# Expert products in 64-row tiles of TensorE, issued in pieces of at most 128 columns

## The chip, the cores and the metric

The kernel runs on one core of a Trainium2 chip. A core has TensorE (PE in the profile; its weight loads are listed apart as PEld), VectorE (DVE), ScalarE (ACT), GpSimd (POOL) and SyncE (SP, which issues most DMAs). The metric is the device time of one execution in microseconds (us), as the median of several runs. Before the change it is 1270.68 us (three runs, 1270.43 to 1271.75).

## The reference, cut to what matters

One transformer block on 2048 tokens of 512 numbers, all in fp32. The result is the sum of three terms: the input, an attention branch and a branch of experts, both fed by the layer-normed input.

```
xn  = layernorm(x)
attention: 16 heads, each with two causal softmax maps; a filter along the tokens; RMS norm; @ Wout
experts:   the gate picks 2 of 8 experts for each token
           routed:  y_e = (silu(xn @ w1[e]) * (xn @ w3[e])) @ w2[e]      (512 -> 352 -> 512)
           shared:  y_s = (silu(xn @ sw1) * (xn @ sw3)) @ sw2            (512 -> 704 -> 512)
out = x + attention + routed (weighted by the gate) + shared
```

Only the order in which the experts' products are issued to TensorE is touched by the change; what is computed is the same.

## The kernel before

The program goes through four stages. First it normalises the tokens, turns them (`xnT`, features on partitions), computes the values `vd`, the gate, the routing and the rotated queries and keys. Then comes `middle`, the longest stage: attention, with the experts' products worked in between. Then `ending` applies the filter, the norm and `Wout`, and gathers the experts' rows. There are two versions of `middle` (lines 1600 to 1605); with the data given, the one without a running maximum runs (`middle(False)`).

**The order of the work in `middle`** is written out by hand: the string `PLAN` (lines 63 to 83) has a letter for each step, and lines 1314 to 1319 carry them out. `S` computes the scores of one unit (line 1067, two matmuls of 64 rows each, for the two maps), after which ScalarE takes the exponential (line 1080) and GpSimd masks the diagonal blocks (line 1089). `V` multiplies the probabilities with the values (line 1111). `U` and `F` sum up and finish a chunk of queries. A lower-case `a` adds probabilities on VectorE (line 1127). `W` advances the experts by one step: `experts` (line 736) is a generator and `W` runs it to its next `yield`. The scores have two PSUM buffers, so a score unit waits for the exponential of the unit but one before it.

**The experts' products** go through `crossing` (line 691). TensorE is used there as two halves: rows 0 to 63 of the contraction (`LO`) and rows 64 to 127 (`HI`) are separate matmuls of 64 rows. Two products are made together, each in a PSUM bank of its own. In a first pass (`n == 0`) the `LO` rows go to the first product while the `HI` rows go to the second. In a second pass (`n == 1`) they change places, so that each product gets both halves, and the two halves never write the same bank at once. Between the passes stands a wait: a ScalarE nop waits for the last matmul of each half of the first pass, and the first matmul of each half in the second pass waits for the nop (`behind`, lines 684 to 689; lines 715 to 719). `passes` (line 726) cuts a crossing into `W` steps of `step` products.

`run(n, a, b)`, line 705, issues the matmuls from product `a` to `b` of a pass: for each `k` one matmul of the `LO` half and one of the `HI` half, with all the columns that the product has. The callers and their moving columns are:

- `wh`, the shared expert's hidden products (line 766): stationary 64 x 128 weights, moving `xnT` with 512 tokens, or 384 in the last group; the sixth chunk has 256, and 256 beside 128 in the last group. One `k` a step.
- `wy`, the shared expert's output (line 826): stationary activations, moving weights with 512 columns, or 256 where a tile is alone. One `k` a step.
- `xu`, a routed expert's hidden products (line 909): stationary 64 x 128 or 64 x 96 weights, moving 128 tokens. Four `k` a step.
- `xy`, a routed expert's output (line 930): moving weights with 256 columns. All three `k` of a pass a step.

In the profile each of these fp32 matmuls appears as two MATMUL rows with two LDWEIGHTS rows. The routed rows come in 34 tiles of 128 slots. 28 of them belong to a single expert and go through `crossing`; six are shared by two experts and go through other functions (`up_half`, line 206, and `down_products`, line 240), which are not touched. The weights of the routed experts are fetched by SyncE into two sets of buffers (`fetch`, `refill`, line 879), each part as soon as TensorE has last read the one before.

Of the kernel before, what the change touches and what calls it, by code (L numbers as in the profile page):

```python
# [20 lines left out]
P = 128  # L21
# [24 lines left out]
LO, HI = slice(0, HALF), slice(HALF, P)  # L46
# [54 lines left out]
def block_kernel(  # L101
# [240 lines left out]
    with ExitStack() as pools:  # L342
# [94 lines left out]
        for c in range(NE):  # L437
            for i in range(NQC):
                nc.tensor.matmul(
                    gt_ps[32 * i : 32 * i + 32, 0, :], gw_sb[:, c, :], xnT[:, c, i * QC : (i + 1) * QC],  # L440
                    start=(c == 0), stop=(c == NE - 1), skip_group_check=True,
# [41 lines left out]
        for t in range(NT):  # L483
# [5 lines left out]
                start=False, stop=(t == NT - 1), skip_group_check=True,  # L489
# [49 lines left out]
        pairs = l1.tile([P, TOP, NT, 2], F32, name="pairs")  # L539
# [27 lines left out]
        _, _, _, _, chunks, _, result = shared_expert(ep, eps)  # L567
# [15 lines left out]
        for st in range(2):  # L583
            for qk in (1, 0):
                if (st, qk) == (1, 1):
                    load_wqk(1, 0, nc.sync)
                for n in range(NQC):
                    cols = slice(n * QC, (n + 1) * QC)
                    ps = lps.tile([P, 2, QC], F32, tag="x", name="ps_x")
                    for i in range(2):  # L590
                        for c in range(NE):
                            nc.tensor.matmul(  # L592
                                ps[:, i, :], wqk_sb[st, qk][:, i, c, :], xnT[:, c, cols],
                                start=(c == 0), stop=(c == NE - 1),
# [49 lines left out]
    def middle(general):  # L644


        with ExitStack() as pools:
# [18 lines left out]
            def bank(shape, name):  # L666


                n = next(n for n in taken if n not in in_pair)
                taken.remove(n)  # L670
                taken.append(n)
                return f_banks.tile(shape, F32, tag=f"f{n}", name=name)
# [11 lines left out]
            def behind(ins, others):  # L684
                for other in others:
                    tc.add_manual_dep(
                        ins.ins, other.ins.name,
                        mybir.DependencyInfo(mybir.DependencyClass.Sync, mybir.DependencyReason.DATA), reason="the other rows",
                    )

            def crossing(shapes, name, first, second=None):

                banks = []
                for shape in shapes:
                    banks.append(bank(shape, name))
                    in_pair.add(taken[-1])  # L700
                pairs = first(banks), second(banks) if second else first(banks)[::-1]
                whole = [max(map(len, each)) for each in pairs]
                last, signal = [None, None], []

                def run(n, a, b):
                    for k in range(a, b):
                        for i, r in enumerate((LO, HI)):
                            side = pairs[n][i]
                            if k < len(side):
                                dst, lhs, rhs = side[k]  # L710
                                last[i] = nc.tensor.matmul(  # L711
                                    dst, lhs[r], rhs[r], start=(n == 0 and k == 0), stop=(n == 1 and k == len(side) - 1),
                                    skip_group_check=True,
                                )
                                if n == 1 and k == 0:
                                    behind(last[i], signal)
                    if b >= whole[n] and n == 0:
                        signal.append(nc.scalar.nop())
                        behind(signal[0], last)
                    elif b >= whole[n]:  # L720
                        in_pair.clear()
                    return banks

                return run, whole

            def passes(run, whole, step):
# [587 lines left out]
            steps = dict(S=score, V=value, U=sum_up, F=finish, T=lambda: turning[0](), W=work, g=fold_step)  # L1314
# [257 lines left out]
    with tc.If(nc.values_load(more[0:1, 0:1], min_val=0, max_val=1) > 0):  # L1572

        with tc.tile_pool(name="before_more", bufs=1) as gap, tc.tile_pool(name="more", bufs=2) as mp, tc.tile_pool(
# [4 lines left out]
            for j in range(NR, NS):  # L1579
# [6 lines left out]
                pairs = both[:, 0]  # L1586
                nc.vector.tensor_add(pairs, pairs, both[:, 1])
                i = mp.tile([P, 1], I32, tag="i", name="i")
# [121 lines left out]
```

## Time and profile before

| | |
|---|---|
| median of the runs | 1270.68 us |
| the profiled execution | 1267.82 us |
| its span, first to last instruction | 1266.1 us |
| granted TensorE clock, mean | 0.998 |
| TensorE matmuls and weight loads | 10954 of each |
| of them from line 711 | 4200: `xu` 2688, `xy` 672, `wh` 576, `wy` 264 |
| chain that ended last, largest parts | `ps_o` L1111 19%, `ps_s` L1067 12%, `xu` L711 12%, `wh` L711 8%, `xy` L711 5%, `wy` L711 4% |

The rows of line 711 by the number of moving columns: 512 columns 540 (`wh` 320, `wy` 200 and 20), 384 columns 160 (`wh`), 256 columns 796 (`wh` 80, `wy` 40 and 4, `xy` 672), 128 columns 2704 (`xu` 2688, `wh` 16).

How to read the profile: times are in us unless marked ns, and count from the start of the span. L711 is line 711 of the kernel; a matmul that a helper issues carries the helper's line, so `wh`, `wy`, `xu` and `xy` are told apart by the tile that they write. In a listing by line, "64*128 64x512 f32 x320 | 79.0, 591" means 64 rows and 128 stationary columns, 64 x 512 moving numbers, 320 times, 79.0 us busy in all, 591 ns mean length of one. Matmuls overlap, and their ends are modelled: the mean length is not the time that one adds, and a busy TensorE is not TensorE at its peak. In a timeline, instructions of one kind that follow each other are merged: start, length of the whole, engine, line, tile, form, count, and in brackets the idle time before with what ended it. In a table of stretches, each engine's busy time is followed by its number of instructions, then come the granted clock, the DMA share and GB/s. The chain that ended last is followed back from the last instruction, at each step to what released it.

`middle` spans about 253 to 1160 us: the shared expert's products (`wh`, `wy`) lie from 253 to 564 us, the single-expert tiles (`xu`, `xy`) from 567 to about 1010 us and, for the last two, from 1126 to 1155 us; the mixed tiles lie between.

### The profile page before, as it was taken

Reading aid. Unit: us, or ns where it says so; the run is one execution under the profiler, and the core shown is the slowest. Engines: PE = TensorE matmul, PEld = TensorE weight load, DVE = VectorE, ACT = ScalarE, POOL = GpSimd, SP = SyncE. Lnnn points to the kernel's source line nnn. Section 1 sums busy time; section 2 is a strip of 40 time slices with the busy share of each in tenths; the row PEclk is TensorE's granted clock in tenths of the full one; section 3 lists DMA queues with packets and bytes.
Section 4 is the critical chain, followed back from the end, with each engine's and each line's share of the span. In section 5 each row is a group of like instructions: output and inputs, shape, how many; then the busy total and the mean of one; then the engine's idle time right before and its main releaser. Section 6 shows DMA issues by size and latency. Waiting matters only on the chain.

```text
span 1266.1 us, 27950 instructions
## 1 busy us (share of the span) xinstructions
PE 1238.9 (98%) x10954; PEld 704.5 (56%) x10954; DVE 997.9 (79%) x1582; ACT 699.7 (55%) x908; POOL 315.5 (25%) x356
## 2 busy tenths in 40 slices
PE   7999999999999999999999999999999999999998
PEld 3444444444544545566777766767766744456544
DVE  7039886177968878878889999999899897776884
ACT  2311111066756667767777778777777756651331
POOL 0001332011111122111221523222222322111875
PEclk9999999999999999999999999999999999999999
DMA  9505867301130122237566566665665669868998
GB/s 370 215 1 147 219 176 173 105 15 34 47 89 20 28 90 72 83 108 233 171 203 225 194 209 200 211 208 171 201 212 186 200 221 332 297 250 271 188 224 188
DMA packets 85782, 214.75 MB, mean 170 GB/s; under 512 B 16788, under 2 KB 17240, under 8 KB 85384
## 3 DMA queue, kind: packets, MB, share of 16 engines
q1 hardware_dynamic: 72920, 185.70, 45.5%
q0 software_dynamic: 11056, 22.78, 8.7%
q10 hardware_dynamic: 1664, 4.38, 1.1%
q8 instruction: 89, 1.46, 0.5%
q14 instruction: 53, 0.43, 0.1%
HBM read 169.69 MB, written 43.10 MB: 168 GB/s over the span
## 4 chain that ended last, share of the span: by engine, by line
PE 75%; DMA 15%; POOL 4%; issue 2%; DVE 1%; ACT 1%; SPq 0%; ACTq 0%; POOLq 0%; DVEq 0%
PE ps_o L1111 19%; PE ps_s L1067 12%; PE xu L711 12%; DMA who<-pairs,slot 11%; PE wh L711 8%; PE xy L711 5%; PE ps_tv L427 5%; PE wy L711 4%; POOL res L1364 3%; PE ps_sum L1144 2%; DMA res<-ysh 2%; PE ps_x L592 2%; PE xy L244 1%; PE xh L210 1%; PE xg L210 1%
## 5 line engine op out<-in xcount | busy, mean ns | idle before, releaser
L1080 ACT ACTIVATE pt<-ps_s 128x1024 f32<-128x1024 f32 x544 | 537.4, 1026 | 201.6 <-PE ps_s L1067 142.7
L1127 DVE TENSOR_TENSOR sum<-sum,pt 128x1024 f32<-128x1024 f32 (+3 forms) x512 | 515.9, 1057 | 45.5 <-ACT pt L1080 22.7
L1089 POOL TENSOR_SCALAR_AFFINE_SELECT pt<-pt 128x256 f32<-128x256 f32 (+1 forms) x224 | 152.9, 703 | 530.0 <-ACT pt L1080 528.9
L1067 PE MATMUL ps_s<-qS,kS 64*128 64x512 f32 (+3 forms) x1280 | 272.9, 476 | 4.1 <-DVEq L1572 1.7
L1111 PE MATMUL ps_o<-pt,vd 128*32 128x512 f32 (+3 forms) x2560 | 262.2, 533 | 1.5 <-POOL pt L1089 1.5
L1067 PEld LDWEIGHTS ps_s<-qS,kS 64*128 64x128 f32 x1280 | 112.8, 186 | 129.6 <-issue 52.9
L711 PE MATMUL xu<-xT,w 64*128 64x128 f32 (+1 forms) x2688 | 168.3, 272 | 0.0
L711 PEld LDWEIGHTS xu<-xT,w 64*128 64x128 f32 (+1 forms) x2688 | 162.1, 178 | 6.7 <-issue 1.8
L1111 PEld LDWEIGHTS ps_o<-pt,vd 128*32 128x32 f32 x2560 | 70.7, 109 | 121.5 <-issue 104.0
L711 PE MATMUL wh<-xnT,w 64*128 64x512 f32 (+3 forms) x576 | 122.6, 523 | 0.0
L592 PE MATMUL ps_x<-xnT,wqk_sb 128*128 128x512 f32 x256 | 110.5, 593 | 0.0
L1132 DVE TENSOR_TENSOR sum<-pt 128x1024 f32<-128x1024 f32 (+1 forms) x64 | 73.9, 1167 | 45.0 <-ACT pt L1080 26.5
L678 POOL DMA_INDIRECT xrow<-xd,tok x34 | 54.3, 1597 | 146.3 <-PE ps_x L861 123.7
L711 PE MATMUL xy<-w,uT 64*128 64x256 f32 x672 | 83.4, 380 | 0.0
L592 PEld LDWEIGHTS ps_x<-xnT,wqk_sb 128*128 128x128 f32 x256 | 48.4, 190 | 60.6 <-issue 60.6
L545 POOL DMA_INDIRECT who<-pairs,slot x32 | 35.1, 1096 | 168.2 <-DVE pairs L542 103.6
L711 PEld LDWEIGHTS wh<-xnT,w 64*128 64x128 f32 x576 | 56.1, 186 | 26.6 <-issue 17.5
L609 ACT CAST hi<-turned 128x1024 fp32r<-128x1024 f32 x16 | 16.7, 1045 | 93.9 <-DVE turned L607 70.9
L711 PEld LDWEIGHTS xy<-w,uT 64*128 64x128 f32 x672 | 62.8, 187 | 7.7 <-DVE vd L1170 0.6
L1364 POOL DMA_INDIRECT res<-ys,slot x32 | 53.6, 1676 | 23.3 <-DMA res<-ysh 11.6
L427 PE MATMUL ps_tv<-wv_sb,xnT 128*128 128x512 f32 x128 | 58.8, 612 | 0.7 <-ACT xnT L424 0.7
L1507 PE MATMUL po<-wo_sb,aT 128*128 128x512 f32 x120 | 54.1, 593 | 0.2 <-ACT aT L1501 0.2
(247 smaller groups left out, 1180.0 us busy)
## 6 DMA issues: line engine op xcount, KB each, us to landing
w<-in_wex_dram SPq DMA_DIRECT2D x88, 704.0 KB, 7.1
w<-in_wex_dram SPq DMA_DIRECT2D x43, 768.0 KB, 5.8
kS<-parts_k SPq DMA_DIRECT2D x256, 64.0 KB, 2.0
qS<-parts_q SPq DMA_DIRECT2D x256, 64.0 KB, 3.0
ys<-y_sb SPq DMA_DIRECT2D x34, 256.0 KB, 4.1
parts_q<-hi SPq DMA_DIRECT2D x32, 256.0 KB, 5.7
parts_k<-hi SPq DMA_DIRECT2D x16, 256.0 KB, 3.5
parts_k<-turned SPq DMA_DIRECT2D x16, 256.0 KB, 6.0
```

The source lines that it names most:

```text
L427: nc.tensor.matmul(pv, xnT[:, c, t * P : (t + 1) * P], wv_sb[:, c, :], start=(c == 0), stop=(c == NE - 1))
L592: nc.tensor.matmul(ps[:, i, :], wqk_sb[st, qk][:, i, c, :], xnT[:, c, cols], start=(c == 0), stop=(c == NE - 1),)
L678: nc.gpsimd.indirect_dma_start(out=x, out_offset=None, in_=xd, in_offset=bass.IndirectOffsetOnAxis(ap=tok[:, j : j + 1], axis=0),)
L711: last[i] = nc.tensor.matmul(dst, lhs[r], rhs[r], start=(n == 0 and k == 0), stop=(n == 1 and k == len(side) - 1), skip_group_check=True,)
L1067: nc.tensor.matmul(to, k, queries[2 * g + h, qc][r, off : off + w], start=True, stop=not general)
L1080: nc.scalar.activation(pt[:, :, used], ps[:, :, used], AF.Exp, scale=SCALE)
L1089: nc.gpsimd.affine_select(out=part, in_=part, pattern=[[0, part.shape[1]], [1, P]], compare_op=ALU.is_ge, fill=0.0, base=0, channel_multip ...
L1111: nc.tensor.matmul(self.o[r : r + 32, off:], vd[:, kb, v0 : v0 + 32], pt[:, s, :], start=first, stop=self.ended, skip_group_check=True,)
L1127: nc.vector.tensor_add(to, to, pt)
L1132: nc.vector.tensor_add(self.sum[h][:, :, m], self.first[h][:, :, m], pt)
L1364: nc.gpsimd.indirect_dma_start(out=came[k], out_offset=None, in_=ys, in_offset=bass.IndirectOffsetOnAxis(ap=slot[:, step - 2, order[k] : o ...
L1507: nc.tensor.matmul(po, aT[:, c, :], wo_sb[:, c, :], start=(c == 0), stop=(c == NE - 1))
```

## The change

In `run`, each matmul is cut along its moving columns into pieces of at most 128 (`P`). The pieces of the two halves go in turn: `LO` columns 0 to 127, `HI` columns 0 to 127, `LO` columns 128 to 255, and so on; where one half has fewer columns, the other goes on alone. Every piece is a matmul with the same stationary operand as the whole had. `start` is set on the first piece of a half's first product only and `stop` on the last piece of the last; the wait for the nop is put on the first piece of the second pass, and `last` holds the last piece issued. `xu`, which has 128 columns already, is issued as before. `PLAN`, the steps and all other code are the same.

```diff
                 def run(n, a, b):
                     for k in range(a, b):
-                        for i, r in enumerate((LO, HI)):
-                            side = pairs[n][i]
-                            if k < len(side):
-                                dst, lhs, rhs = side[k]
+                        steps = [(i, r, *pairs[n][i][k]) for i, r in enumerate((LO, HI)) if k < len(pairs[n][i])]
+                        for j in range(0, max(rhs.shape[-1] for *_, rhs in steps), P):
+                            for i, r, dst, lhs, rhs in steps:
+                                m = slice(j, min(j + P, rhs.shape[-1]))
+                                if m.start >= m.stop:
+                                    continue
                                 last[i] = nc.tensor.matmul(
-                                    dst, lhs[r], rhs[r], start=(n == 0 and k == 0), stop=(n == 1 and k == len(side) - 1),
+                                    dst[:, m], lhs[r], rhs[r, m], start=(n == 0 and k == 0 and j == 0),
+                                    stop=(n == 1 and k == len(pairs[n][i]) - 1 and m.stop == rhs.shape[-1]),
                                     skip_group_check=True,
                                 )
-                                if n == 1 and k == 0:
+                                if n == 1 and k == 0 and j == 0:
                                     behind(last[i], signal)
```

## The prediction, made before the result was known

> **What bounds the kernel now.** I read the page first, then the stages, then the forms of the changed line, then the matmuls one by one.
>
> The head of the page (engine, busy us, share of the span, instructions) and the chain that ended last:
>
> ```profile
> PE 1238.9 (98%) x10954; PEld 704.5 (56%) x10954; DVE 997.9 (79%) x1582; ACT 699.7 (55%) x908; POOL 315.5 (25%) x356
> ...
> PE 75%; DMA 15%; POOL 4%; issue 2%; DVE 1%; ACT 1%; SPq 0%; ACTq 0%; POOLq 0%; DVEq 0%
> ```
>
> TensorE is busy throughout and the chain lies on it. A busy PE need not be working at its peak, so the stages come next: busy time by engine from 250 to 565 us (shared expert beside attention) and from 565 to 1020 us (routed experts beside attention).
>
> ```profile
> 250.00:565.00 315.00, 311.77 (x2614) 158.53 (x2616) 251.92 (x309) 215.20 (x250) 57.22 (x84) 1.00 0.19 56
> 565.00:1020.00 455.00, 453.14 (x6090) 319.78 (x6082) 413.23 (x690) 337.49 (x455) 126.31 (x146) 1.00 0.63 203
> ```
>
> In both, PE lacks 3.2 and 1.9 us of being always busy, the granted clock is 1.00, and VectorE (252 of 315, 413 of 455) and ScalarE have room. What PE takes longer there, the end gets later by.
>
> The forms of the changed line 711 (rows x stationary columns, then moving rows x columns, count, busy us, mean ns):
>
> ```profile
> L711 PE MATMUL xu<-xT,w 64*128 64x128 f32 x1792 | 114.2, 273 | 0.0
> ...
> L711 PE MATMUL xy<-w,uT 64*128 64x256 f32 x672 | 83.4, 380 | 0.0
> L711 PE MATMUL wh<-xnT,w 64*128 64x512 f32 x320 | 79.0, 591 | 0.0
> L711 PE MATMUL xu<-xT,w 64*96 64x128 f32 x896 | 58.8, 270 | 0.0
> ```
>
> The kernel already holds the form that the change makes of everything: xu, in 128 columns, 1792 times. Each product is two MATMUL rows and each row has its own LDWEIGHTS (10954 of both in all). The durations (591 and 273) overlap, so the price is the pace, read from the timeline (start, length, engine, line, count): a stretch in which score pairs (L1067) and runs of wh alternate, and one in which score pairs and runs of xu do.
>
> ```profile
> 279.67 1.02 PE L711 MATMUL wh<-xnT,w 64*128 64x512 f32 x4
> ...
> 280.75 1.02 PE L711 MATMUL wh<-xnT,w 64*128 64x512 f32 x4
> ...
> 281.84 1.02 PE L711 MATMUL wh<-xnT,w 64*128 64x512 f32 x4
> ```
>
> ```profile
> 654.75 1.05 PE L711 MATMUL xu<-xT,w 64*128 64x128 f32 x16
> ...
> 655.53 0.19 PEld L1067 LDWEIGHTS ps_s<-qS,kS 64*128 64x128 f32 x2
> 655.56 0.48 PE L1067 MATMUL ps_s<-qS,kS 64*128 64x512 f32 x2
> ...
> 655.88 1.04 PE L711 MATMUL xu<-xT,w 64*96 64x128 f32 x16
> ```
>
> Four wh rows of 512 and a score pair take (281.84 - 279.67) / 2 = 1.085 us. Sixteen xu rows of 128, the same number of columns, and a score pair take 655.88 - 654.75 = 1.13 us. That is the change in miniature: 0.045 us more for two pairs of 512, 22 ns a pair (a pair is one row from each half).
>
> **The change part by part.**
>
> *Columns streamed.* The same before and after; the two halves run side by side in both. In a run of wh the loads of successive pairs start at 384.15 and 384.58 us, and those of the score pair behind them at 385.01: 430 ns a pair of 512.
>
> ```profile
> 384.15 0.21 PEld L711 LDWEIGHTS wh<-xnT,w 64*128 64x128 f32 x2 [0.22 <-issue]
> 384.58 0.21 PEld L711 LDWEIGHTS wh<-xnT,w 64*128 64x128 f32 x2 [0.22 <-issue]
> 385.01 0.21 PEld L1067 LDWEIGHTS ps_s<-qS,kS 64*128 64x128 f32 x2 [0.22 <-issue]
> ```
>
> Loads lie idle 0.22 us between pairs ("issue": nothing to wait for but the stream). This slack is what the change fills.
>
> *Instructions added.* Line 711 has 540 rows of 512 columns (wh 320, wy 200 and 20), 160 of 384 (wh) and 796 of 256 (wh 80, wy 44, xy 672). They become 2160, 480 and 1592: 2736 more matmuls and 2736 more loads, each load with the weights that its half already held. xu stays as it is.
>
> *Pace of the pieces.* In the xu run of 16 above, the last of 8 pairs starts (1.05 - 0.27) us after the first (0.27 is the mean row), 0.78 / 7 = 111.5 ns a pair. Loads run without a gap there, so stream and load are about equally long and little hides the rest. Against that:
> - 512: 4 x 111.5 - 430 = 16 ns a pair within a run, 22 with its ends (the 1.13 against 1.085). I take 18; 270 pairs give 4.9 us.
> - 384: a run of 12 wh rows at 476.43 us lasts 2.10 us, less one row (0.49) over 5 steps is 322 ns a pair; 3 x 111.5 - 322 = 12.5 ns, 80 pairs, 1.0 us.
> - 256: loads in xy runs start 215.5 to 217 ns apart (12 rows in 1.46 us, less 0.376, over 5); 2 x 111.5 - 216 = 7 to 7.5 ns, 398 pairs, 3.0 us.
>
> Sum: **8.9 us** of PE time, 6.3 of it before 565 us (wh, wy) and 2.6 after (xy).
>
> *Bounds of the pace.* What no row shows is 128-column pieces that load the same weights again. From below: the xu rows with 96 stationary columns, whose loads are shorter (160 against 188 ns), go 16 rows in 1.04 us, (1.04 - 0.27) / 7 = 110 ns a pair; by that the sum is 270 x 10 + 80 x 8 + 398 x 4 = 4.9 us. Zero would need loads that are left out, and every row has one; that is a rival below. From above: 22 ns for 512 with run ends, and 16 and 10 in proportion for the others: 5.9 + 1.3 + 4.0 = 11.2 us. I stay near the plain 128-column rows, which differ from the new pieces in nothing but the weights.
>
> *A rule against the change.* The trace has 55.8 ns a row of 128 columns and 215 ns a row of 512 (half a pair's pace), nearly a ratio of 4. The Trainium skill, "TensorE: Matmul & The Clock Gate", section "Back-to-back issue gap", gives about 81 ns a matmul sustained at 128 columns and 131 at 512. By that page a row of 512 cut in four would cost 4 x 81 - 131 = 193 ns more, and 540 of them 104 us, as an estimate; no run here shows such a price, and the xu rows speak against it.
>
> *Waits.* The wait between the two passes of a crossing stays on the first piece, and the ScalarE nop still waits for the last; nothing new is queued behind it. Pieces behind the first need no wait, since PE goes in order. The order of all other work and of every DMA stays; weight fetches wait for the last reader on PE, so they move with it.
>
> *What lies beside other work.* PE's idle time in the middle is the cover: 3.2 + 1.9 us by the stages, of which 1.7 lie ahead of the first wide product (253 us) and 0.8 just behind it (256 us), where hardly any delay has built up. Of the remaining 2.6, spots where PE waits for GpSimd's mask or ScalarE's exp, and of the weight wait after 1117 us (which moves along, because PE triggers those fetches), I count 0.6 us as taken up. The tail after 1160 us starts from the last stored expert row and moves along.
>
> **Sum.** 8.9 - 0.6 = +8.3 us. The profiled execution took 1267.82 us (span 1266.1 and 1.7 outside), so the like of it would be 1276.1; it lies 2.9 below the median of the runs, so the forecast stands on that: 1270.68 + 8.3 = **1279.0 us**.
>
> **Rivals.**
> 1. *Repeated weights are cheap.* The program might not reload what a half already holds, or the load might hide. For: no row shows a reload of the same weights. Against: every MATMUL row has its own load. The pieces then cost between nothing and the 4.9 us of the 110 ns pace: 1270.7 to 1275.6, about half of it within what counts as no change.
> 2. *Faster: the halves are not really side by side.* If the ends of the rows (which are modelled) hide that one half of a wide run lags by a row, 430 ns, with the other half of the array idle at its ends, pieces of 128 would cut the lag to 111.5: 0.32 us a run. I count 208 runs of wide products in the timeline, so up to 67 us less: 1279 - 67 = 1212 us. Against it: taking the pairs out of the two periods above leaves 1.085 - 2 x 0.43 = 0.225 us for the score pair beside wh and 1.13 - 8 x 0.1115 = 0.24 beside xu; a lag would leave 0.32 more beside wh. It decides from 8.9 / 208 = 43 ns of lag a run on.
> 3. *Dearer: instructions.* PE gets 25% more of them, 0.35 MB to fetch. The instruction queue carries 1.46 MB in 89 packets of 16 KB now, so 21 more; if each held PE up for 0.5 to 1 us (the size of PE's present waits), +10 to +21 on top: 1289 to 1300. Against: xu runs hold 4 instructions in 111.5 ns, 36 a us, for the 2.7 us of 48 rows without a gap.
>
> **How the numbers follow.** The forecast's case (1276 to 1282): 0.74. Cheap reload: 0.13, of which 0.06 within no change. Faster: 0.05. Dearer: 0.08. The range leaves out the last two and the 0.06: 1273 to 1283, which holds both bounds of the pace (4.9 - 2.6 gives 1273.0, 11.2 gives 1281.9). With 0.2% (2.5 us, about what a measurement of this kernel tells from no change): faster 0.05, same 0.06, slower 0.89.
>
> **What the changed profile would show.** PE at x13690; line 711 with 128 columns only, 6936 rows; pairs 111 to 112 ns apart in wh runs too, with loads that no longer idle 0.22 us; the exp's period beside wh 1.125 instead of 1.085; the shared expert's stage some 6 us longer, the routed one's some 2.5, the mixed pairs and the tail unchanged but later. Wrong would be: fewer loads than matmuls, a wh pace above 115 ns, gaps on PE with no releaser, or a stage before 565 us that gets shorter.

## The result, and the profile after

The changed kernel takes 1280.1 us (median of 6 runs, 1277.46 to 1282.01), the kernel before 1270.05 in the runs beside it: a ratio of 1.0076, 95% interval 1.0062 to 1.0091. That is 10 us more, by the interval 7.9 to 11.6. A second set of runs (below) gives 1.0064 (1.0050 to 1.0077), so the cost is some 8 to 10 us. The forecast was 1279.0, 8.3 over the median it started from.

The profiled execution took 1278.31 us, 1276.6 of it span. The head of its page, and the queue that brings TensorE's instructions among others:

```profile
PE 1247.4 (98%) x13690; PEld 801.3 (63%) x13690; DVE 997.1 (78%) x1582; ACT 699.8 (55%) x908; POOL 312.2 (24%) x356
...
q8 instruction: 111, 1.82, 0.6%
```

There are 2736 more matmuls and as many more loads, and 22 more packets of instructions. VectorE and ScalarE do what they did. TensorE's busy time grew by 8.5 us, that of the loads by 97 us: the loads filled time that had been free.

The two stages with the changed products, cut at the first `wh`, the first `xu` and the first product of a mixed tile (busy us and number of each engine, then clock, DMA share, GB/s). Before:

```profile
253.24:567.12 313.88, 312.39 (x2633) 158.74 (x2631) 252.75 (x308) 215.97 (x251) 57.04 (x82) 1.00 0.19 56
567.12:1020.60 453.48, 451.62 (x6067) 319.14 (x6063) 411.71 (x689) 336.77 (x453) 125.41 (x145) 1.00 0.63 203
```

After:

```profile
254.17:573.54 319.37, 318.10 (x4698) 242.54 (x4697) 252.83 (x309) 216.11 (x251) 56.27 (x82) 1.00 0.20 56
573.54:1028.88 455.34, 453.73 (x6690) 330.97 (x6687) 410.69 (x689) 336.66 (x453) 124.58 (x145) 1.00 0.62 202
```

The shared expert's stage is 5.5 us longer, the routed one's 1.9. In both, PE's busy time grew by a little more than the stage (5.7 and 2.1), while VectorE's, ScalarE's and GpSimd's stayed within 1.1 us: little of the cost was taken up, and PE's idle time did not grow (1.5 and 1.9 us before, 1.3 and 1.6 after). The granted clock is 1.00 in all four.

The price itself, in the timeline after, at the place that corresponds to the stretch at 280 us before (`wh` is issued on line 713 now, the score pairs on line 1070):

```profile
281.19 1.05 PE L713 MATMUL wh<-xnT,w 64*128 64x128 f32 x16
...
282.00 0.47 PE L1070 MATMUL ps_s<-qS,kS 64*128 64x512 f32 x2
282.08 1.09 PEld L713 LDWEIGHTS wh<-xnT,w 64*128 64x128 f32 x16
282.31 1.05 PE L713 MATMUL wh<-xnT,w 64*128 64x128 f32 x16
...
283.43 1.05 PE L713 MATMUL wh<-xnT,w 64*128 64x128 f32 x16
```

Sixteen rows of 128 columns and a score pair now take 1.12 us (281.19, 282.31, 283.43), where four rows of 512 and a score pair took 1.085. The loads run through, 16 in 1.09 us; the 0.22 us in which they lay idle between pairs are gone. The pair of pieces starts every (1.05 - 0.27) / 7 = 111.5 ns, as `xu` does.

### The profile page after: what moved, and what is told of

The parts are those of the page before. It is cut to its first block, busy times and chain, and to the rows that moved or that the text cites. A ratio compares the mean times of both kernels' runs of the same rounds, so it can differ in the third digit from the quotient of the medians.

```text
span 1276.6 us, 33408 instructions
## 1 busy us (share of the span) xinstructions
PE 1247.4 (98%) x13690; PEld 801.3 (63%) x13690; DVE 997.1 (78%) x1582; ACT 699.8 (55%) x908; POOL 312.2 (24%) x356
## 4 chain that ended last, share of the span: by engine, by line
PE 68%; DMA 4%; POOL 4%; issue 2%; DVE 1%; ACT 1%; SPq 0%; POOLq 0%; DVEq 0%; ACTq 0%
PE ps_o L1114 18%; PE ps_s L1070 12%; PE xu L713 12%; PE wh L713 8%; PE xy L713 5%; PE wy L713 4%; POOL res L1367 3%; PE ps_sum L1147 2%; DMA res<-ysh 2%; PE xy L244 1%; PE xh L210 1%; PE xg L210 1%; DMA res<-ys,slot 1%; DMA w<-in_wex_dram 1%; PE ps_x L864 1%
## 5 line engine op out<-in xcount | busy, mean ns | idle before, releaser
L1070 PE MATMUL ps_s<-qS,kS 64*128 64x512 f32 (+3 forms) x1280 | 234.4, 417 | 4.0 <-DVEq L1575 1.7
L1070 PEld LDWEIGHTS ps_s<-qS,kS 64*128 64x128 f32 x1280 | 109.2, 186 | 92.6 <-ACT pt L1083 36.4
L713 PEld LDWEIGHTS wh<-xnT,w 64*128 64x128 f32 x1936 | 124.1, 188 | 5.1 <-issue 0.8
L713 PE MATMUL wh<-xnT,w 64*128 64x128 f32 x1936 | 126.4, 272 | 0.0
L713 PE MATMUL xy<-w,uT 64*128 64x128 f32 x1344 | 85.6, 274 | 0.0
L713 PEld LDWEIGHTS xy<-w,uT 64*128 64x128 f32 x1344 | 81.9, 188 | 2.5 <-DVE vd L1173 0.6
L713 PE MATMUL wy<-w,ws 64*128 64x128 f32 x880 | 55.7, 273 | 0.0
```

Source lines behind the costliest of these rows:

```text
L713: last[i] = nc.tensor.matmul(dst[:, m], lhs[r], rhs[r, m], start=(n == 0 and k == 0 and j == 0), stop=(n == 1 and k == len(pairs[n][i]) - ...
L1070: nc.tensor.matmul(to, k, queries[2 * g + h, qc][r, off : off + w], start=True, stop=not general)
```

## The experiments

For each profile I cut the span at the same six instructions: first `wh`, first `xu`, first mixed-tile product, first `xu` after those, last `xy`, end. All in us; "before" is three profiles (the first one and the two repeats told of below); the second row has the changed kernel's first profile, its repeat, and the run with new weights in each piece.

| kernel | ahead | shared | routed | mixed | last two | tail |
|---|---|---|---|---|---|---|
| before | 253.2, 254.2, 253.9 | 313.9, 314.0, 313.8 | 453.5, 453.5, 453.5 | 105.7, 106.7, 106.4 | 28.0, 28.0, 28.0 | 111.8, 111.9, 113.8 |
| changed; again; new weights | 254.2, 253.1, 254.6 | 319.4, 319.2, 319.4 | 455.3, 455.2, 455.3 | 105.8, 105.7, 106.5 | 28.6, 28.6, 28.6 | 113.3, 113.7, 113.3 |
| pieces of 256 | 254.4 | 314.9 | 453.4 | 107.5 | 28.7 | 112.2 |
| 128 in wh, wy only | 252.9 | 319.4 | 453.3 | 104.3 | 28.4 | 113.9 |
| 128 in xy only | 254.0 | 314.0 | 455.4 | 104.5 | 28.3 | 112.8 |
| one half first | 253.8 | 360.1 | 458.5 | 106.2 | 28.8 | 114.6 |
| 64 in wh, wy | 253.8 | 479.6 | 456.4 | 108.3 | 28.6 | 112.0 |
| two and two | 254.1 | 322.8 | 458.4 | 106.4 | 28.8 | 112.1 |

The stages shared and routed repeat within 0.2 us. The stretches ahead, mixed and tail vary by 1 to 2 us between executions of the kernel before, and by up to 4 across all the rows, so single us of the total are read from the stages.

### The changed kernel again

No edit.

> The changed kernel once more, beside the others. My account (pace: a pair of 128-column pieces takes 111.5 ns where 512 columns took 430 and 256 took 216) gives some 8 us over the kernel before, all of it between the first shared-expert product and the last routed one; the +0.9 us ahead of them and the +1.5 us behind them that the first profile shows would be chance and not come again. If they belong to the change, both come again and the time is 10 us over.

Measured: 1277.3 us, ratio 1.0064 (1.0050 to 1.0077), +7.6 on the medians. The stages repeat (319.2 and 455.2). The 0.9 us ahead did not come again (253.1), the long tail did (113.7).

### Pieces of 256

```diff
+                        wide = 2 * P
-                        for j in range(0, max(rhs.shape[-1] for *_, rhs in steps), P):
+                        for j in range(0, max(rhs.shape[-1] for *_, rhs in steps), wide):
...
-                                m = slice(j, min(j + P, rhs.shape[-1]))
+                                m = slice(j, min(j + wide, rhs.shape[-1]))
```

> Pieces of at most 256 columns in turn, so 540 rows of 512 become 1080 of 256, 160 of 384 become 160 of 256 and 160 of 128, and xy stays whole. Pace: 270 pairs x (2 x 216 - 430) = 0.5 us and 80 x (216 + 111.5 - 322) = 0.4 us, about +1 us over the kernel before. Rival (each added matmul and load costs by its number, as instruction supply would): 700 of 2736 rows are added, 26% of 10 us, +2.6 us.

Measured: 1272.59 us, ratio 1.0021 (1.0013 to 1.0030), +2.9 on the medians, by the interval 1.7 to 3.8. By the total the rival's 2.6 fits better than 1. By the stages it does not: all the added rows lie in the shared stage, which is 1.0 us longer (314.9 against 313.9), as the pace has it. In the changed kernel 2064 added rows make this stage 5.5 us longer; by their number 700 would make it 1.9 longer. The stage repeats within 0.2 us, so this one profile speaks for the pace. The routed stage did not grow (453.4). What the total has beyond 1.0 us lies in the stretches that vary (mixed 107.5) and in the last two tiles (28.7); what brought it there is open.

### 128 columns in wh and wy only, and in xy only

```diff
+                        wide = P if name in ("wh", "wy") else E      # the other run: P if name == "xy" else E
-                        for j in range(0, max(rhs.shape[-1] for *_, rhs in steps), P):
+                        for j in range(0, max(rhs.shape[-1] for *_, rhs in steps), wide):
...
-                                m = slice(j, min(j + P, rhs.shape[-1]))
+                                m = slice(j, min(j + wide, rhs.shape[-1]))
```

> 128-column pieces for wh and wy only; xy keeps 256. Pace: the shared expert's stage is as long as in the changed kernel (319.4 us, 5.5 over before), the routed stage as before (453.5), together +5.5 to +6.3 us. Rival (number of instructions): 2064 of 2736 rows, 75% of 10 us, +7.5 us.

> 128-column pieces for xy only; wh and wy stay whole. Pace: the shared expert's stage as before (313.9 us), the routed stage as in the changed kernel (455.3, 1.9 over before), +2 to +2.6 us in all. Rival (number of instructions): 672 of 2736 rows, 25% of 10 us, +2.5 us; this run alone does not tell them apart, its stages and the sum with the run on wh and wy do.

Measured: 1273.61 us, ratio 1.0034 (1.0021 to 1.0046) for `wh` and `wy`; 1271.39 us, 1.0019 (1.0007 to 1.0031) for `xy`. The stages come out as the account by pace says, each in its place: 319.4 and 453.3 us in the first, 314.0 and 455.4 in the second. The two costs simply add up: 5.5 and 1.9 us by the stages, as in the changed kernel (by the medians 3.9 and 1.7, against 7.6 for the changed kernel in the same set, with intervals of some 3 us each). These two runs do not separate the rivals. The 7.5 us that the number of instructions was said to cost in the first run rest on 10 us for the whole; of the 7.6 in this set 75% are 5.7, inside the interval of 2.7 to 5.8. And by the stages an added row costs 2.7 ns in `wh` and `wy` (5.5 us / 2064) and 2.8 in `xy` (1.9 / 672). It is the runs with pieces of 256 and of 64 that speak against a price per row.

### One half first

```diff
-                        for j in range(0, max(rhs.shape[-1] for *_, rhs in steps), P):
-                            for i, r, dst, lhs, rhs in steps:
+                        cuts = range(0, max(rhs.shape[-1] for *_, rhs in steps), P)
+                        for each in steps:
+                            for j in cuts:
+                                i, r, dst, lhs, rhs = each
```

> Pieces of 128 columns, but all pieces of one half ahead of all of the other instead of in turn. Theory A (TensorE takes its matmuls in program order, a half runs beside the other only where the two follow each other): of 512 columns cut in four, only the last piece of one half and the first of the other can overlap, so a pair of 512 takes up to about 780 ns instead of 446, +90 us on 270 pairs, +16 on 80 pairs of 384 and +45 on 398 of 256: about +150 us over the changed kernel. Theory B (the order within a pair does not matter, because enough pieces are in flight): within 3 us of the changed kernel.

Measured: 1323.36 us, ratio 1.0431 (1.0411 to 1.0452). Both theories fail as they stand. The order matters, by 40.7 us in the shared stage and 3.2 in the routed one. Theory A's sum lets nothing overlap but the two halves of one product; by that the shared stage would lose some 115 us (90, 18 rather than 16 for 384 columns, and 7 for the 62 pairs of 256). But in strict order, too, the last piece of one product can run beside the first of the next (or beside a score pair that stands between). Then a step of 512 columns, two rows for each piece, takes 12 rows' time for 8, one of 384 columns 8 for 6, and one of 256 nothing more: 135 x 4 x 0.1115 + 40 x 2 x 0.1115 = 69 us in the shared stage, and next to nothing for `xy`. So the routed stage does not speak against strict order; the 40.7 us and the starts of the rows do. The timeline (score pairs are on line 1072 here, the pieces on 715):

```profile
284.00 1.27 PE L715 MATMUL wh<-xnT,w 64*128 64x128 f32 x13
285.01 0.50 PE L1072 MATMUL ps_s<-qS,kS 64*128 64x512 f32 x1
285.11 0.50 PE L715 MATMUL wh<-xnT,w 64*128 64x128 f32 x4
285.37 0.48 PE L1072 MATMUL ps_s<-qS,kS 64*128 64x512 f32 x1
285.45 1.16 PE L715 MATMUL wh<-xnT,w 64*128 64x128 f32 x12
```

The two rows of a score pair, which started together, are 0.36 us apart (285.01 and 285.37): one half of TensorE runs ahead by three to four rows. In the single rows of the trace the first product of this stretch starts with 4 rows alone (284.002, 284.115, 284.224 and 284.336), then two rows together (284.448 and 284.453), one alone, two more pairs, and 5 alone. Rows of one half follow each other every 0.11 us, so two that start together lie in different halves. So the second half starts when the first half's third piece does, as its fifth row starts; in strict order it could not start before the fourth piece, the seventh row.

### Pieces of 64

```diff
+                        wide = HALF if name in ("wh", "wy") else P
```

(used as in the run with pieces of 256)

> Pieces of 64 columns for wh and wy, 128 for xy. Theory A (the weight load sets a floor: loads of 128 columns come no closer than some 107 to 112 ns a pair, however short the matmul): a pair of 512 columns takes 8 x 111 = 890 ns instead of 446, +120 us on 270 pairs, +27 on 80 pairs of 384, +14 on 62 of 256, about +160 us over the changed kernel. Theory B (each piece costs its columns, 0.84 ns each, and a fixed 4 ns): a pair of 64 columns takes 58 ns, +5 us over the changed kernel.

Measured: 1446.66 us, ratio 1.1403 (1.1343 to 1.1463); the shared stage is 479.6 us, 160 more than in the changed kernel, as theory A says. The timeline, pieces of half the columns:

```profile
281.69 3.68 PE L714 MATMUL wh<-xnT,w 64*128 64x64 f32 x64
285.18 0.48 PE L1071 MATMUL ps_s<-qS,kS 64*128 64x512 f32 x2
285.49 1.89 PE L714 MATMUL wh<-xnT,w 64*128 64x64 f32 x32
```

32 pairs in 3.68 us, less one row of 0.27, over 31 steps: 110 ns a pair (in the single rows 112, after a first step of 55), the same as with 128 columns. So here the pace does not come from the moving columns. It could come from the loads, or from a fixed price of each row or pair, and other lines of the same profile tell these apart:

```profile
383.01 0.89 PEld L1148 LDWEIGHTS ps_sum<-sum,pick 128*32 128x32 f32 x32
383.12 1.06 PE L1148 MATMUL ps_sum<-sum,pick 128*32 128x128 f32 x32
...
394.56 0.39 PEld L1160 LDWEIGHTS ps_ot<-cst,o_sb 64*128 64x128 f32 x8
394.67 0.42 PE L1160 MATMUL ps_ot<-cst,o_sb 64*128 64x64 f32 x8
```

`ps_sum` takes four rows, each with its own load of 32 columns, in (1.06 - 0.27) / 7 = 113 ns, and `ps_ot` (transposes) two rows of 64 columns in the two halves, with their loads, in some 65 ns. A fixed price of 55 ns a row, or of 110 ns a pair, is refuted. What remains is the load. Its recorded length goes with the stationary columns, 110 ns for 32 (`ps_sum`), 160 for 96 and 188 for 128 (`xu`), which is 0.81 ns a column and an estimate of 104 ns for 128. For these products, then, a pair goes no faster than its two loads, side by side. It is not so for every load of 128 columns: those of the transposes last 138 ns and come every 65.

The Trainium skill, "TensorE: Matmul & The Clock Gate", section "LDWEIGHTS (loading the stationary operand)", has columns / 1.2 ns for a load, by which 128 columns take 107 ns, as an estimate. The 110 to 112 measured for the products here come near it, if the loads of the two halves run side by side; the transposes, at some 65, do not agree with it.

### New weights in each piece

The pieces of `xy` go through the three products of a pass for the first 128 columns, then for the next.

```diff
-                    for k in range(a, b):
+                    cuts = range(0, max(rhs.shape[-1] for side in pairs[n] for *_, rhs in side), P)
+                    for j, k in [(j, k) for j in cuts for k in range(a, b)]:
...
-                        for j in range(0, max(rhs.shape[-1] for *_, rhs in steps), P):
```

> As the changed kernel, but xy, whose three products of a pass stand in one step, goes piece by piece through the three products, so that each load brings other weights than the one before it on its half; wh and wy, with one product a step, are as in the changed kernel. If a repeated load of the same weights costs what any load costs, the time is that of the changed kernel within 1 us and xy pairs stay 111 to 112 ns apart. If the repetition itself costs or saves something, the routed stage moves by 336 pairs x 2 pieces x that.

Measured: 1278.0 us, ratio 1.0071 (1.0055 to 1.0088); the routed stage is 455.3 us, as in the changed kernel, and pairs of `xy` rows start 112 ns apart in both. To load the same product's weights again for the next piece costs what it costs to load another product's. The trace does not say whether the two rows of one product load the same numbers, so whether a half was ever given exactly what it held is not shown.

### The kernel before, twice more

No edit.

> The kernel before, profiled once more, for the stretches that no change touches. By the first profiles the changed kernel has +0.9 us ahead of the first shared product (254.2 against 253.2) and +1.5 us behind the last routed one (113.3 against 111.8). If that is chance, the two new profiles of before spread over 253 to 254.5 and 111.8 to 114 as the changed kernels do; if it belongs to the change, both stay at 253.2 and 111.8.

> The same once more: chance spreads the stretches ahead and behind, the stages between stay at 313.9 and 453.5 us within 0.3.

Measured, one execution each: 1270.16 and 1271.1 us. Ahead 254.2 and 253.9, tail 111.9 and 113.8, while the stages stay at 314.0, 313.8 and 453.5: chance moves the stretches ahead and behind by as much as the first two profiles differed there.

### Two and two

```diff
-                        for j in range(0, max(rhs.shape[-1] for *_, rhs in steps), P):
-                            for i, r, dst, lhs, rhs in steps:
+                        cuts = range(0, max(rhs.shape[-1] for *_, rhs in steps), 2 * P)
+                        for each, j in [(each, j) for o in cuts for each in steps for j in (o, o + P)]:
+                            if True:
+                                i, r, dst, lhs, rhs = each
```

> Pieces of 128 columns, two of one half, two of the other, and so on. The run with one half first cost the shared expert's stage 40.7 us but xy, which has two pieces a half, only some 3. Theory A' (each half can hold one matmul waiting behind the one that runs, and only when it is full does the other half's next one wait): two and two costs the same as in turn, 319.4 us for the shared stage, 1278 in all. Theory A (strict order, overlap only between neighbours): a product of 512 columns takes 5 slots of two pieces' rows for 4, 0.22 us more on 135 products, some +30 us.

Measured: 1284.5 us, ratio 1.0118 (1.0067 to 1.0169). The shared stage is 322.8 us, 3.4 more than in turn: not 30, but not nothing. The 30 leave out that the last pieces of one product can run beside the first of the next; with that, strict order also fills both halves, so this run does not tell strict order from one waiting matmul a half. For `xy`, with two pieces a half, the order is the same as in the run with one half first, and the routed stage is the same (458.4 and 458.5). The timeline:

```profile
281.49 1.06 PE L715 MATMUL wh<-xnT,w 64*128 64x128 f32 x15
282.30 0.47 PE L1072 MATMUL ps_s<-qS,kS 64*128 64x512 f32 x1
282.39 0.27 PE L715 MATMUL wh<-xnT,w 64*128 64x128 f32 x1
282.42 0.47 PE L1072 MATMUL ps_s<-qS,kS 64*128 64x512 f32 x1
282.61 1.06 PE L715 MATMUL wh<-xnT,w 64*128 64x128 f32 x15
```

Within a run of half-row work the period is 1.12 us (281.49 to 282.61), that of the changed kernel; but one half is a row ahead of the other (the score rows start 0.12 us apart). The lag has to be made up each time TensorE turns to work on all 128 rows. In the changed kernel's trace I count 31 such turns after `wh` and `wy` in the shared stage; 31 x 0.1115 is 3.5 us, against 3.4 measured. In the routed stage 33 give 3.7 against 3.2. That the turns are where it is lost is worked out, not tried by itself.

## Why the prediction was right

- **What bounds the kernel.** TensorE's time passes to the end. Shown: in both stages the added busy time of PE and the added length agree within 0.3 us, and by the stages two parts tried alone add up.
- **The pace of the pieces.** Forecast 111.5 ns a pair, from the rows of another product; measured the same in `wh`, `wy` and `xy`. Why it is so, and no faster, the 64-column run and its other lines show: it is the pace of these products' loads. That each load brings weights which its half already held, as the prediction has it, is not shown. A pair of 512 columns cost 16 to 17.5 ns more ((1.12 - 1.085) / 2) for the 18 that I took.
- **The sizes.** 6.3 us were forecast for `wh` and `wy` and 2.6 for `xy`, less 0.6 absorbed. Measured by the stages, three profiles of each kernel: 319.3 - 313.9 = 5.4, 455.3 - 453.5 = 1.8, and 0.6 in the last two tiles, where kernels with a whole `xy` also show 0.4 to 0.7 more; 7.8 in all for 8.3. PE's busy time grew by 5.7 and 2.0 us in the same profiles, so some 0.5 us was taken up, where 0.6 was forecast. The terms were a little large: with 16 ns a pair of 512 in place of 18, and 7 a pair of 256, `wh` and `wy` come to 5.8 by the same sum, and `xy` comes to 2.0 us / 312 pairs = 6.5 ns, not 7.5. A share of the 0.6 in the last two tiles may be chance.
- **What is left of the total.** The medians have +10.0, +7.6 and, with new weights in each piece, +9.5 us in three sets; the stages have 7.8. The total of 1280.1 lies 1.1 from the forecast, but single us of it are not told from chance. The rest lies in stretches that the repeats of the kernel before show to vary. Whether the changed kernel's tail (113.3 to 113.7 in three profiles, against 111.8 to 113.8) is longer by up to 1 us stays open.
- **The rival of the halves that lag.** Refuted for the kernel before: the pieces shortened neither stage, and in its single rows the two halves' rows of `wh` with 512 columns start 4 ns apart (median of 160 pairs, none over 121), where the rival needs 430, or 43 to decide. The runs with other orders show what a lag looks like, and that order can bring one.
- **The rival of cheap reloads.** Refuted: each piece has its load (13690 of both), and loads for a next piece cost the same with the product's own weights and with another's.
- **The rival of the instructions.** 22 more packets came, and PE's idle time in the two stages did not grow. A price per row fits the runs on `wh` and `wy` and on `xy` alone, at 2.7 and 2.8 ns, but not the shared stage with pieces of 256 (+1.0 us, not 1.9), nor that with pieces of 64, whose 5000 added rows cost 166 us, 33 ns each.
- **The rule that spoke against the change**, an estimate of 104 us from the 81 and 131 ns of the Trainium skill, "TensorE: Matmul & The Clock Gate", section "Back-to-back issue gap", is more than ten times too dear: the rows show 56 ns for 128 columns (half of 111.5) and 215 for 512. The forecast rightly stayed with the rows.

## What to carry to other kernels

A matmul is cut for free only as long as its columns take longer than its load: here the two halves' loads of 128 columns go at 110 to 112 ns a pair, which 128 fp32 columns (430 / 4 = 107.5 ns) just fall short of, so pieces of 256 cost next to nothing, pieces of 128 some 4%, pieces of 64 double the time. The price of a new form could be read here from a product in the same kernel that has it already; compare whole periods of the stream rather than mean durations, since matmuls overlap. A price per added row and a price by pace can fit the same totals: look for a run in which the two differ. Where a product is split over the two halves of the rows, issue the halves in turn: four pieces of one half ahead of the other cost the shared stage 40.7 us, two and two 3.4.

## What the runs showed that was not expected

The order of two halves is looser than strict. In the program each fp32 product is one instruction, and its two rows in the trace come from that one. With all pieces of one half first, the other half's first piece, issued behind the fourth, starts beside the third. It looks as if each half holds one matmul that waits behind the one that runs, and only a third holds up what follows. That is not shown: the rows carry no mark of their half, the account was not worked through to the 40.7 us, and the run with two and two fits strict order as well. The Trainium skill, "TensorE: Matmul & The Clock Gate", section "Part 3: Packing small matmuls — row/col tiling", says that matmuls start and end strictly in program order. By that the second half would start no earlier than the first half's seventh row, and the shared stage would lose at least 69 us, as worked out above; here it starts beside the fifth, with 40.7 us.
